# Side work between attention steps: where variances, output projections and a sort's operations stand in the queues

## The chip, the cores and the metric

The kernel runs on one core of one Trainium2 chip, in one launch. The metric is the time on the device in microseconds. The time before is the median of nine runs. One execution was also recorded by the profiler, and every duration below comes from it.

## The reference

The input has B = 2 images of C = 256 channels and 56 x 56 places, that is N = 3136 tokens of 256 numbers each, all float32. The computation, cut to what matters:

```python
x = relu(batchnorm(conv_nonlocal(x)) + x)         # layer 0: grouped non-local block
t = to_tokens(x)                                  # (2, 3136, 256)
q, k, v = split(layernorm(t) @ W_attn)            # 4 heads of 64
att = softmax(causal(q @ k.T / 8))
t = t + (att @ v) @ W_proj                        # causal attention
z = layernorm(t)
p = softmax(z @ gate_w + gate_b)                  # 8 experts
w, e = top_k(p, 2)                                # two experts for each token
t = t + sum(w[j] * (gelu(z @ W1[e[j]]) @ W2[e[j]]) for j in (0, 1))
```

## The kernel before

**Stages.** Layer 0 takes the first 100 us or so. Then comes causal attention, about 775 us, first over batch 0 and then over batch 1. The last 455 us are the experts' stage: tokens are sorted by expert, and 102 blocks of 128 rows go through their expert's two matrices, batch 0's blocks first.

**Attention.** Queries are cut into 7 blocks of W = 448 (index i). The four heads go in two pairs (hp). So each batch has 14 sections, written here (b, i, hp), and 28 in all. Within a section, `attend` walks over the key chunks j of 128 keys that the causal mask leaves. One key chunk is one step:

- `scores` (L669) makes a tile `sc` on TensorE (PE). ScalarE (ACT) takes its exponential into `st` (L677). If the chunk lies on the diagonal, VectorE (DVE) multiplies the edge by a 0/1 mask (L679). DVE adds `st` to a running sum `acc` (L687 for the first, L691 for the rest).
- `values` (L709) multiplies `st` by the values into `yp`, three steps later (`LAG = 3`).

Steps on the diagonal ("cut" in the code) have fewer columns, and each is followed by a full step as long as there are some. They stand at a section's end. `sc` has two buffers, `st` five.

When the scores of a section's last step have been issued, `visit(i, hp)` runs, then `sum_rows`, whose four matmuls `sp` (L733) sum `acc` over the partitions. The sums go out and back through DRAM on SP's queue (L741, L744), are inverted (L753, L754), broadcast (L759) and multiplied into the head's result (L765); `later` holds these tasks with the step at which they are due. At the start of the next section GpSimd (POOL) adds the two halves of `yp` (L721).

**Work at a visit.** `ahead` gives the projections for the next query block as pieces: after hp = 0 four `query_key` pieces (qk, L549) with the copies of `qT` and `kT` (L557), after hp = 1 up to four `value` pieces (v, L566, copies L575); and the transposes of normalised tokens (xp, L535, copied to `px` at L541; POOL normalises them, L520) for the block after that. After batch 0's last block these are pieces of batch 1. Each piece of PE takes a PSUM bank from `pm`, which has two, used in turn; so does `sp`. A piece therefore waits until the piece two before it has been copied out.

**Side work.** For each batch a generator `tokens` yields between pieces: `project_gate` once; `project_out`, which for two chunks of 128 tokens multiplies the attention's result by W_proj (pp, L619), adds it to the tokens on DVE (L624), stores them for batch 0 (L626) and takes mean and variance (`stats`, L177 and L178); then `dispatch`, the sort by expert: Newton steps for the reciprocal deviation (L998 to L1001), softmax, two largest, ranks and slots, some 60 small DVE operations, and at last 25 scatters: DVE makes the rows (L1303), POOL issues two indirect DMAs for each (L1311). `bg` gives these rows two buffers. After batch 0's sort the experts' first matrices are loaded (L1795). `apart` and `op` in `dispatch` only yield.

A generator yields `True` after work, `False` where it must wait for something, and `"pe"` just before work for PE. `pull(n)` advances the first generator in `queue` that can go on, until n of them have yielded `True`; one that yields `"pe"` is held back until `products()` advances it. With `every=True`, in the experts' stage, `"pe"` is passed over. The manual schedule issues instructions in just this order on each engine; each engine works through its queue in order.

Before, every second step calls `pull(2)`, and a visit is: all projections, then twice `pull()` and `products()`, then the transposes, then `sp`.

Of the kernel before, what the change touches and what calls it, by code (L numbers as in the profile page):

```python
# [28 lines left out]
def conv_attn_moe_kernel(  # L29
# [52 lines left out]
    P = 128  # L82
    B, C, N = x.shape
# [8 lines left out]
    NCH = -(-N // P)  # L92
    W = 448
# [79 lines left out]
    def stats(b, n, m, k, pool, nm):  # L173

        for a in range(m):
            st6 = pool.tile([P, 6], F32, tag="st6", name=f"st6_{nm}_{n}_{a}")
            nc.vector.bn_stats(st6[:k], ts[b][:k, n + a, :C])  # L177
            nc.vector.bn_aggr(ts[b][:k, n + a, MEAN : MEAN + 2], st6[:k])  # L178
# [9 lines left out]
    with tc.tile_pool(name="c_w", bufs=1) as cw, tc.tile_pool(name="c_s", bufs=2) as cs, tc.tile_pool(  # L188
# [170 lines left out]
        first = fold(0, gram(0, iter(())))  # L359
# [98 lines left out]
    def layer1(nm, general):  # L458

        with ExitStack() as whole:  # L460
# [4 lines left out]
            bg = pool(whole, "bg", bufs=2)  # L465
# [143 lines left out]
            def project_out(b, qT, done):  # L609

                for first, m, k in pairs():
                    while done() < (first + m - 1) * P + k:
                        yield False
                    yield "pe"
                    for n in range(first, first + m):
                        o = n * P
                        ps = bank(f"pp_{b}_{n}")
                        for c in range(NH):
                            nc.tensor.matmul(  # L619
                                ps[:k, : C + E], qT[:, c, o : o + k], wpr[:, c, :],  # L620
                                start=(c == 0), stop=(c == NH - 1),
                            )
                        t = ts[b][:k, n, : C + E]
                        nc.vector.tensor_tensor(t, t, ps[:k, : C + E], ALU.add)  # L624
                        if b == 0:
                            nc.sync.dma_start(out=rest_d[:k, n], in_=t[:, :C])  # L626
                    stats(b, first, m, k, bg, f"o{nm}{b}")

                    for _ in range(3 if b else 1):
                        yield True  # L630

            def attend(
                b, qT, kT, v, fst, fs, psc, py, visit, between, clock, later, finished
# [4 lines left out]
                steps, firsts = [], {}  # L638
                for i in range(NB):
                    nk = -(-((i + 1) * W) // P)  # L640
                    whole_js = [j for j in range(nk) if (j + 1) * P - 1 <= i * W]
                    cut = [j for j in range(nk) if j not in whole_js]
# [136 lines left out]
                for n in range(len(steps) + LAG):  # L779
                    if 0 < n <= len(steps) and steps[n - 1][4]:  # L780
                        i, hp = steps[n - 1][:2]
                        visit(i, hp)
                        sum_rows(hp, i)
                    if n < len(steps):
                        i = steps[n][0]
                        between(i, ends[i] - n)

                    late = n >= LAG and steps[n - LAG][3]
                    if n >= LAG:
                        due(clock[0])  # L790
                        clock[0] += 1
                    if n >= LAG and not late:
                        values(n - LAG)
                    if n < len(steps):
                        scores(n)
                    if late:
                        values(n - LAG)
# [154 lines left out]
            def dispatch(b):  # L952

                t = ts[b]
                tail = chunk(NCH - 1)
                ops = [0]

                def small_piece():

                    if b:  # L960
                        yield True
# [5 lines left out]

                def op():

                    ops[0] += 1  # L970
                    for _ in range(0 if b else 1 + ops[0] % 2):
                        yield True

                def small(name, last=E, dt=F32):
# [2 lines left out]
                def wide(ap):  # L977
# [8 lines left out]
                    small(k, 1).rearrange("p t o -> p (t o)") for k in ("newton_x", "newton_y", "red")  # L986
                )
                nc.vector.tensor_scalar(x, var, 1e-5, None, ALU.add)
                nc.vector.tensor_scalar(
                    y.bitcast(I32), x.bitcast(I32), 1, None, ALU.arith_shift_right  # L990
                )
                nc.vector.tensor_scalar(
                    y.bitcast(I32), y.bitcast(I32), -1.0, float(0x5F3759DF), ALU.mult, ALU.add
                )
                yield from small_piece()
                for i in range(4):
                    to = var if i == 3 else y
                    nc.vector.tensor_tensor(z, y, y, ALU.mult)  # L998
                    nc.vector.tensor_tensor(z, z, x, ALU.mult)
                    nc.vector.tensor_scalar(z, z, -0.5, 1.5, ALU.mult, ALU.add)  # L1000
                    nc.vector.tensor_tensor(to, y, z, ALU.mult)  # L1001
                    yield from op()
                    yield from small_piece()
# [28 lines left out]
                left = small("left")  # L1032
# [77 lines left out]
                first = few("first")  # L1110
# [187 lines left out]
                for n in range(NCH):  # L1298
                    kk = chunk(n)
                    xr = (scatter_rows[0] if b else bg).tile(  # L1300
                        [P, width], F32, tag="xr", name=f"xr_{nm}{b}_{n}"
                    )
                    nc.vector.tensor_scalar(  # L1303
                        xr[:kk, :C], t[:kk, n, :C],
                        t[:kk, n, MEAN : MEAN + 1], t[:kk, n, RSTD : RSTD + 1],
                        ALU.subtract, ALU.mult,
                    )
                    if b:
                        nc.vector.tensor_copy(xr[:kk, C:], t[:kk, n, C + E - 2 : SLOT + 1])  # L1309
                    for k in range(2):  # L1310
                        s = nc.gpsimd.indirect_dma_start(  # L1311
                            out=xds[b],
                            out_offset=bass.IndirectOffsetOnAxis(ap=idxs[b][:kk, k, n : n + 1], axis=0),
                            in_=xr[:kk],
                            in_offset=None,
                            bounds_check=xds[b].shape[0] - 1,
                            oob_is_err=False,
                        )
                        group = f"x_slots_{nm}{b}"
                        tc.declare_no_dep(s.ins, group=group, reason="different rows")  # L1320
                        tc.add_to_no_dep_group(group, s.ins)
                        if b or k:
                            yield True
                    if b == 0:
                        yield False
                sent[b] = True

            def experts(w1s, w2s, b2s, ex, es, ps6, between, need, written, settle, decide):
# [420 lines left out]
            def advance(g):  # L1749
                held.discard(g)  # L1750
                r = next(g, None)
                if r is None:
                    queue.remove(g)
                elif r == "pe":
                    held.add(g)
                return r

            def pull(n=1, every=False):

                while n > 0:  # L1760
                    for g in list(queue):
                        if g in held and not every:
                            continue
                        r = advance(g)
                        while r == "pe" and every:
                            r = advance(g)
                        if r is None or r is True:
                            n -= r is True
                            break
                    else:  # L1770
                        return

            def products():

                for g in list(queue):
                    if g in held:
                        advance(g)
                        return
# [88 lines left out]
            else:  # L1867
# [26 lines left out]
                for b in range(B):  # L1894
                    queue.append(tokens(b, qT, lambda b=b: min(finished[b])))

                    def visit(i, hp):

                        now, then = ahead(b, i, hp)
                        for piece in now:  # L1900
                            piece()
                        for _ in range(2):
                            pull()
                            products()
                        for piece in then:
                            piece()

                    def between(i, left):
                        if b == B - 1 and i == NB - 1:

                            now = load_w2(left < NCH - 4)
                            for _ in range(1 if left > NCH - 4 else 2):
                                next(now, None)

                        tick[0] += 1
                        if tick[0] % 2:
                            pull(2)

                    due = attend(
                        b, qT, kT, v, fst, fs, psc, py, visit, between,  # L1920
                        clock, later, finished[b],
                    )
# [250 lines left out]
```

## Time and profile before

| | |
|---|---|
| median of 9 runs | 1330.9 us (1328.14 to 1336.74) |
| profiled execution, its own time | 1331.52 us |
| its span, first to last instruction | 1329.8 us |
| mean granted TensorE clock | 0.991 |
| layer 1's attention | about 100 to 875 us |
| the experts' stage | about 875 to 1330 us |
| batch 0's scatters (L1303) | 689.7 to 776.0 us |

Times in the profile count from the first instruction. A line of a group or of the timeline names the source line, the engine, the operation, what it writes and reads, and in brackets how long the engine stood idle before it and what ended that.

### The profile page before, as it was taken

What the parts mean: (1) busy time and instruction counts of PE and PEld (TensorE: products, weight loads), DVE (VectorE), ACT (ScalarE), POOL (GpSimd) and SP (SyncE); (2) the same over time, 40 slices, a digit from 0 to 9 for tenths busy, and PEclk for the clock granted to TensorE, in tenths of its full rate; (3) what the DMA queues carried; (4) which work ended last, traced back from release to release, by engine and by line L of the source; (5) the groups of instructions that cost most, each with busy time, mean ns of one, the idle gap of its engine ahead of it and who ended that gap; (6) DMA issues with size and microseconds to landing.
All of it is one profiled execution on the core that took longest, in us unless ns stands there. A gap on an engine that the chain in (4) does not pass through costs nothing. (4 is left out here: it accounts for less than half of the span.)

```text
span 1329.8 us, 28093 instructions
## 1 busy us (share of the span) xinstructions
PE 1272.5 (96%) x10589; PEld 829.6 (62%) x10589; DVE 795.2 (60%) x1665; ACT 609.7 (46%) x1227; POOL 349.4 (26%) x317
## 2 busy tenths in 40 slices
PE   8998999999999999999999899999999899899997
PEld 7875445544444555444444344579978799798896
DVE  1582567667777745766877687764754343354564
ACT  0144555555656554555554456543422233243442
POOL 1112330000002223311126630000066212665561
PEclk9999999999999999999999999999989899899999
DMA  9994101000000001000002233321244333465554
GB/s 296 384 350 133 23 17 32 24 9 24 9 16 9 25 1 28 21 16 9 16 23 81 73 138 96 103 72 54 67 134 140 116 112 97 144 186 184 178 172 132
DMA packets 111182, 124.49 MB, mean 94 GB/s; under 512 B 19686, under 2 KB 100823, under 8 KB 111040
## 3 DMA queue, kind: packets, MB, share of 16 engines
q1 hardware_dynamic: 97216, 93.44, 22.8%
q0 software_dynamic: 9840, 25.67, 5.7%
q10 hardware_dynamic: 3984, 3.50, 0.8%
q8 instruction: 87, 1.43, 0.4%
q14 instruction: 55, 0.45, 0.1%
HBM read 62.71 MB, written 61.05 MB: 93 GB/s over the span
## 5 line engine op out<-in xcount | busy, mean ns | idle before, releaser
L677 ACT ACTIVATE st_f<-sc_f 128x896 f32<-128x896 f32 (+5 forms) x400 | 330.5, 840 | 226.0 <-PE sc_f L669 194.3
L691 DVE TENSOR_TENSOR acc_f<-acc_f,st_f 128x896 f32<-128x896 f32 (+5 forms) x372 | 379.9, 1021 | 73.4 <-ACT st_f L677 58.8
L669 PE MATMUL sc_f<-qT_f,kT_f 64*64 64x448 f32 (+6 forms) x3184 | 340.4, 500 | 10.1 <-ACT st_f L677 7.2
L709 PE MATMUL yp_f<-st_f,v_f 64*64 64x448 f32 (+6 forms) x3184 | 342.1, 501 | 4.0 <-DVE st_f L679 2.6
L1442 ACT ACTIVATE g_f<-ht_f,b1b 128x128 f32<-128x128 f32 x408 | 116.9, 371 | 255.6 <-PE ht_f L1433 123.3
L669 PEld LDWEIGHTS sc_f<-qT_f,kT_f 64*64 64x64 f32 x3184 | 121.1, 133 | 164.8 <-issue 122.9
L709 PEld LDWEIGHTS yp_f<-st_f,v_f 64*64 64x64 f32 x3184 | 120.3, 133 | 156.7 <-issue 133.7
L1433 PE MATMUL ht_f<-xT_f,w_f 128*128 128x128 f32 x1632 | 207.2, 278 | 9.9 <-issue 8.8
L1433 PEld LDWEIGHTS ht_f<-xT_f,w_f 128*128 128x128 f32 x1632 | 200.5, 194 | 18.3 <-issue 13.0
L721 POOL TENSOR_TENSOR qT_f<-both_f 128x448 f32<-128x448 f32 x28 | 37.0, 1321 | 493.0 <-ACT both_f L720 492.9
L1311 POOL DMA_INDIRECT x_slots<-xr_f,idx x100 | 111.0, 1110 | 146.2 <-DVE xr_f L1309 101.5
L1421 DVE COPY w_f<-w1s_f 128x1024 f32 x102 | 72.1, 708 | 90.2 <-PE ht_f L1433 35.3
L520 POOL TENSOR_SCALAR xn_f<-t 128x256 f32<-128x256 f32 (+1 forms) x50 | 80.3, 1612 | 171.3 <-PE xp_f L535 66.2
L1473 POOL DMA_INDIRECT y_tokens<-ys_f,to_f x57 | 58.2, 1021 | 128.9 <-DVE ys_f L1462 103.9
L1462 DVE TENSOR_TENSOR ys_f<-yp_f,kT_f 128x128 f32<-128x128 f32 x102 | 29.6, 290 | 101.8 <-PE yp_f L1452 74.9
L549 PE MATMUL qk_f<-px_f,wat 128*128 128x512 f32 (+2 forms) x224 | 88.1, 546 | 1.2 <-ACT px_f L541 1.2
L549 PEld LDWEIGHTS qk_f<-px_f,wat 128*128 128x128 f32 x224 | 40.6, 190 | 46.9 <-issue 41.6
L679 DVE TENSOR_TENSOR st_f<-st_f,keep 128x256 f32<-128x256 f32 (+1 forms) x112 | 45.6, 407 | 34.4 <-ACT st_f L677 33.2
L687 DVE COPY acc_f<-st_f 128x896 f32<-128x896 f32 x28 | 17.7, 634 | 79.4 <-ACT st_f L677 79.1
L1452 PE MATMUL yp_f<-kT_f,g_f 128*128 x204 | 62.3, 387 | 1.3 <-issue 1.3
L1452 PE MATMUL yp_f<-px_f,g_f 128*128 x204 | 62.4, 388 | 0.9 <-issue 0.7
L1452 PE MATMUL yp_f<-v_f,g_f 128*128 x204 | 61.5, 383 | 0.9 <-issue 0.9
(273 smaller groups left out, 1270.3 us busy)
## 6 DMA issues: line engine op xcount, KB each, us to landing
x_slots<-fill SPq DMA_DIRECT2D x1, 8190.0 KB
xb_f<-x_slots SPq DMA_DIRECT2D x60, 130.0 KB
x_slots<-fill SPq DMA_DIRECT2D x1, 7296.0 KB
y_slots<-ys_f SPq DMA_DIRECT2D x57, 128.0 KB
kept<-t SPq DMA_DIRECT2D x2, 3200.0 KB
x<-in_x_dram SPq DMA_DIRECT2D x14, 448.0 KB
rb_f<-inverses SPq DMA_DIRECT2D x56, 112.0 KB
xr<-in_x_rows_dram SPq DMA_DIRECT2D x12, 512.0 KB
```

What stands on the lines that cost most here:

```text
L520: nc.gpsimd.tensor_scalar(xn[:k, a], ts[b][:k, n + a, :C], ts[b][:k, n + a, MEAN : MEAN + 1], ts[b][:k, n + a, RSTD : RSTD + 1], ALU.subtr ...
L549: nc.tensor.matmul(ps[:, :w], wat[:, c, d0 : d0 + P], px[:, s % 2, c, :w], start=(c == 0), stop=(c == NH - 1),)
L669: nc.tensor.matmul(ps[h : h + HS, a, c0:W], kT[hp][rows, j * P + h : j * P + h + HS], qT[rows, hp, q0 + c0 : q0 + W], start=True, stop=True,)
L677: nc.scalar.activation(st[:k, :, c0:], ps[:k, :, c0:W], AF.Exp, scale=SCALE)
L691: nc.vector.tensor_tensor(acc[:k, :, c0:], acc[:k, :, c0:], st[:k, :, c0:], ALU.add)
L709: nc.tensor.matmul(yp[a * HS : (a + 1) * HS, h // HS, c0:W], v[hp][h : h + HS, j, a, :HS], st[h : h + HS, a, c0:], start=first, stop=bool( ...
L1311: s = nc.gpsimd.indirect_dma_start(out=xds[b], out_offset=bass.IndirectOffsetOnAxis(ap=idxs[b][:kk, k, n : n + 1], axis=0), in_=xr[:kk], i ...
L1421: nc.vector.tensor_copy(w, w1s[:, :, bass.ds(e, 1), :].rearrange("p c e h -> p c (e h)"))
L1433: nc.tensor.matmul(ht[:, k, :], w[:, c, k * P : (k + 1) * P], xT[:, c, :], start=(c == 0), stop=(c == NH - 1),)
L1442: nc.scalar.activation(g[:, k, :], ht[:, k, :], AF.Gelu, bias=b1bs[b][:, k, i : i + 1])
L1452: nc.tensor.matmul(yp[:, :C], g[:, k, :], w2s[k][:, bass.ds(e, 1), :].rearrange("p e d -> p (e d)"), start=(k == 0), stop=(k == KH - 1),)
L1473: s = nc.gpsimd.indirect_dma_start(out=y_tokens, out_offset=bass.IndirectOffsetOnAxis(ap=to[:, n % GB : n % GB + 1], axis=0), in_=ys, in_o ...
```

## The change

The order of issue changes, and nothing else: both programs hold the same instructions.

- The variances leave `project_out`. A new generator `closer` for each pair of chunks is put at the head of the queue; each pull takes one chunk's mean and variance. `project_out` ends when all are taken, and no longer yields `True` after each pair, so a second `products()` can follow at once with the next pair.
- A visit issues all but the last two projections, then `products()` once or twice, then the last but one projection, the transposes, and the last projection. It no longer pulls. Without projections (last block) `products()` stands before and after the transposes.
- `between` pulls one piece at every step, except in block i = 0, whose steps all lie on the diagonal; before, two at every second step.
- `op` in `dispatch` yields once for batch 0, where it yielded once and twice in turn; and it stands after each of Newton's operations, which went four at a time.
- After each scatter of batch 0, `dispatch` yields `True` where it yielded `False`: a scatter takes two pulls, and the next generator in the queue is not reached.
- In the experts' stage a pull passes over one `"pe"` and counts a second.

In the new order a visit reads, with a batch's two output projections as an example: qk qk pp pp pp pp qk xp qk sp, where it was qk qk qk qk pp pp pp pp xp sp.

```diff
-                    stats(b, first, m, k, bg, f"o{nm}{b}")
-
-                    for _ in range(3 if b else 1):
-                        yield True
+                    queue.appendleft(closer(b, first, m, k))
+                while unclosed[b]:
+                    yield False
+
+            unclosed = [NCH] * B
+
+            def closer(b, first, m, k):
+
+                for n in range(first, first + m):
+                    stats(b, n, 1, k, bg, f"o{nm}{b}")
+                    unclosed[b] -= 1
+                    yield True
...
-                        between(i, ends[i] - n)
+                        between(i, ends[i] - n, (steps[n][2] + 1) * P > i * W + 1)
...
                 def op():
 
-                    ops[0] += 1
-                    for _ in range(0 if b else 1 + ops[0] % 2):
+                    if b == 0:
                         yield True
...
                     nc.vector.tensor_tensor(z, y, y, ALU.mult)
+                    yield from op()
                     nc.vector.tensor_tensor(z, z, x, ALU.mult)
+                    yield from op()
                     nc.vector.tensor_scalar(z, z, -0.5, 1.5, ALU.mult, ALU.add)
+                    yield from op()
                     nc.vector.tensor_tensor(to, y, z, ALU.mult)
                     yield from op()
...
                     if b == 0:
-                        yield False
+                        yield True
...
                         r = advance(g)
-                        while r == "pe" and every:
+                        if r == "pe" and every:
                             r = advance(g)
+                            r = True if r == "pe" else r
...
                         now, then = ahead(b, i, hp)
-                        for piece in now:
+                        for piece in now[:-2]:
                             piece()
-                        for _ in range(2):
-                            pull()
+                        products()
+                        if now:
                             products()
-                        for piece in then:
+                        for piece in now[-2:-1] + then + now[-1:]:
                             piece()
-
-                    def between(i, left):
+                        if not now:
+                            products()
+
+                    def between(i, left, cut):
...
                         tick[0] += 1
-                        if tick[0] % 2:
-                            pull(2)
+                        if not cut or i:
+                            pull()
```

More of the change, by code (lines that the diff above doesn't have):

```diff
@@ L955, in dispatch @@
                 tail = chunk(NCH - 1)
-                ops = [0]
                 def small_piece():
@@ L998, in dispatch @@
                     nc.vector.tensor_tensor(z, y, y, ALU.mult)
+                    yield from op()
                     nc.vector.tensor_tensor(z, z, x, ALU.mult)
+                    yield from op()
                     nc.vector.tensor_scalar(z, z, -0.5, 1.5, ALU.mult, ALU.add)
+                    yield from op()
                     nc.vector.tensor_tensor(to, y, z, ALU.mult)
```

## The prediction

> **What bounds the kernel now.** I read busy time and the chain of waits first, then the clock by windows, then what PE waits for. The chain ends at an ACT copy with 0% shares, so it tells nothing. Busy time does:
>
> ```profile
> PE 1272.5 (96%) x10589; PEld 829.6 (62%) x10589; DVE 795.2 (60%) x1665; ACT 609.7 (46%) x1227; POOL 349.4 (26%) x317
> ```
>
> PE bounds the kernel, and the change neither adds nor removes an instruction on any engine: in the order of the two programs each line occurs equally often, on equal shapes. Only PE's idle time can move. Windows by stage (PE, PEld, DVE, ACT, POOL busy, clock, DMA):
>
> ```profile
> 100.00:500.00 400.00, 392.40 (x3740) 191.55 (x3739) 251.85 (x373) 222.65 (x343) 65.08 (x43) 1.00 0.09 27
> 500.00:690.00 190.00, 183.48 (x1736) 87.50 (x1738) 131.03 (x249) 103.10 (x168) 36.10 (x22) 1.00 0.07 16
> 690.00:800.00 110.00, 101.14 (x1014) 44.25 (x1006) 79.64 (x125) 55.31 (x79) 62.06 (x52) 1.00 0.28 95
> 800.00:875.00 75.00, 73.85 (x800) 35.52 (x792) 57.67 (x73) 43.08 (x52) 2.49 (x2) 1.00 0.30 88
> 875.00:1330.00 455.00, 428.97 (x2847) 391.69 (x2843) 225.30 (x682) 161.97 (x540) 168.94 (x161) 0.97 0.42 131
> ```
>
> The first four are attention: 775 us with 24.1 us idle at full clock. The last is the experts' stage, 26 us idle, with three stretches of 6.8 us at clock 0.50 (989.1:995.9 and two more); of the change only the second batch's projections and sort reach it, one block of tokens sooner or later. Attention's waits:
>
> ```profile
> PE sc_f L669 <- ACT st_f L677: 7.2, 8, 1.5
> PE yp_f L709 <- DVE st_f L679: 2.6, 5, 1.0
> PE sp_f L733 <- DVE t L624: 2.3, 3, 1.2
> PE xp_f L535 <- DVE t L624: 2.2, 6, 1.2
> PE sc_f L669 <- issue: 1.7, 3, 0.9
> PE sp_f L733 <- ACT kT_f L557: 1.5, 6, 0.3
> PE sp_f L733 <- ACT v_f L575: 0.9, 3, 0.3
> ```
>
> A wait costs more than it prints. Score matmuls print 0.98 us but the next values start 0.75 us later (453.33 to 454.08), so 0.16 to 0.23 us of modelled tail hides part of each; I add 0.16.
>
> Write (b,i,hp) for a section: batch, query block, head pair; its visit follows it.
>
> **Bunched sort and variances, gain 0.9.** At visit (1,1,1) DVE receives 22 side operations in a row:
>
> ```profile
> 548.13 0.42 DVE L177 BATCH_NORM_STATS2 st_of<-t 64x6 f32<-64x256 f32 x1
> ...
> 549.45 0.19 DVE L998 TENSOR_TENSOR red_f<-newton_y_f 128x25 f32<-128x25 f32 x1
> ...
> 550.21 0.76 DVE L624 TENSOR_TENSOR t<-t,pp_f 128x264 f32<-128x264 f32 x2
> 550.77 0.63 PE L535 MATMUL xp_f<-ident,xn_f 128*128 128x128 f32 x4 [1.16 <-DVE t L624]
> ```
>
> L624 empties the PSUM bank that the transposes need. Variances and Newton steps stand ahead of it, seven of Newton's at 0.19 alone. After, the three L624 come first and variances follow one chunk a step: 1.16 + 0.16 = 1.3 goes. Next late is the last value product (below), 0.4 (0.3 + 0.16, less what overlaps). Gain 0.9. What hides the moved variances is DVE's slack in full steps: 1.50 us of PE against 1.09 of L691, 0.41 for 0.56 (starts 548.13 to 548.59, and the aggregate); the 0.15 short per step falls into the lag of three steps between scores and values. Without it: 0.15 a step, up to 4 steps in eight visits, 5.
>
> **Projections amid the others, 0.2.** Five other visits put transposes behind L624: (2.2 - 1.2) / 5 = 0.2, with tail 0.36 each. Four of these go, since no variance stands between the L624s any more; (0,6,0) has no input projection and keeps its own. But bank order decides what comes: two banks alternate, and with one transpose pair (about 0.5 us) between the last two projections, the last waits for the copy of the one before it: kT 0.25 (1.5 / 6) + 0.16 = 0.4, v 0.3. Three visits exchange 0.36 for 0.4, one for 0.3, and (1,4,1) its sum's wait for px, 0.4 + 0.16, for 0.3: 0.2. Behind the new wait stand, on PE, the sum and the next section's values and scores, and for those ACT waits; so it costs in full. The other two of sp's waits on L624 (2.3 - 1.2 = 1.1, at (1,6,0) and (1,6,1)) become those of a third projection, two pairs standing there now: 0.
>
> **Transposes before the last projection, none, then -0.7.** Where no output projection stands, the sum (sp) waits 0.4 or 0.3 today because transposes are shorter than the copy; after, the last projection waits the same for the same reason. At (0,6,1) two transpose pairs come before the last value: two waits, 0.3 more each way, I take -0.4. Visit (1,5,1) loses its projections, and its sum then follows a value product, as at (0,5,1): -0.3. Moving the gate's transposes and product to two visits removes wg's 0.7 + 0.16 and adds two copies' waits of 0.4: 0.
>
> **Sorting on diagonal steps, gain 2.3.** In sections (1,2,0) to (1,4,1) values wait for the masked tile:
>
> ```profile
> 642.96 0.62 DVE L765 TENSOR_TENSOR qT_f<-qT_f,rb_f 128x448 f32<-128x448 f32 x1
> 643.49 0.42 DVE L679 TENSOR_TENSOR st_f<-st_f,keep 128x256 f32<-128x256 f32 x1
> 643.97 0.66 PE L709 MATMUL yp_f<-st_f,v_f 64*64 64x256 f32 x8 [0.66 <-DVE st_f L679]
> ```
>
> Sum 2.6 + 5 x 0.16 = 3.4. The order shows in (1,2,0) four Newton operations ahead of one mask become one; in (1,3,0) three wide ones (L1042, L1045, L1047: 0.36, 0.36, 0.8) leave the diagonal and L1021 (0.35) comes; in (1,3,1) 0.36 + 0.59 leave and 0.36 + 0.36 + 0.8 come earlier, so its wait stays; (1,4,0) gains some. I leave 1.1: gain 2.3, from -1 to 3.4.
>
> **Scatter, gain 2.9.** 25 pieces (L1303 on DVE, two L1311 on POOL at 0.97 + 0.30) went one per two steps plus up to two a visit; now one per two steps only, 25 in 48 steps. At 690-800 scores wait 5.1 us for ACT in six places; one cause is in the DVE queue:
>
> ```profile
> 757.06 0.41 DVE L1303 TENSOR_SCALAR xr_f<-t 128x256 f32<-128x256 f32 x1 [2.38 <-DMA x_slots<-xr_f,idx]
> 757.87 0.59 PE L733 MATMUL sp_f<-acc_f,ones 128*32 128x224 f32 x8 [1.19 <-DVE t L624]
> ```
>
> L1303 waits for its buffer, and the projections, then the sum, wait behind it. Visit (1,5,0) has no projection now, nor extra pieces: 1.19 + 0.16 = 1.35 goes. Of the six waits (6.1 with tails) I let 1.5 go, from -3.5 (a diagonal more inside the scatter) to 4 (POOL drained during each visit). Instruction waits ("issue") stay.
>
> **SP, -0.4.** w1's eight loads of 512 KB move from (1,5,1) into (1,6,0), spread by two steps. Behind two of them and five of w2 queue the broadcasts that L765 needs; that wait was 1.6 us and cost PE nothing. Bounds 0 and -2. The last is issued at step 17 of (1,6,0), about 50 us before the experts begin at 875. SP's other issues keep their order but for one pair of stores of rest, one section later. Projections moved into the experts' stage cost PE the same there, on other banks' slack: 0.
>
> **Sum.** 0.9 + 0.2 - 0.7 + 2.3 + 2.9 - 0.4 = 5.2. The profiled execution took 1331.5 us (span 1329.8), 0.6 above the median of 1330.9: 1331.5 - 5.2 = 1326.3, and, set against the median, a little under it. I say 1326.
>
> [...] An operation of 25 elements took 1.13 us, six times its usual, beside POOL's addition:
>
> ```profile
> 556.68 1.25 POOL L721 TENSOR_TENSOR qT_f<-both_f 128x448 f32<-128x448 f32 x1 [12.82 <-ACT both_f L720]
> 556.84 1.13 DVE L998 TENSOR_TENSOR red_f<-newton_y_f 128x25 f32<-128x25 f32 x1
> ```
>
> [...] By the rows L721 comes in full steps, where DVE has 0.41 us to spare and three steps of lag, and already catches L691 there (1.4 us in most sections) without a wait of PE; I charge nothing.
>
> **Rivals.** *Waits change places only* (0.30): the bank waits are an exchange, and the diagonals keep theirs because L765 and the mask meet as before. Left is 1.35 + 0.9 - 0.7 = 1.55: 1330. For it: (1,3,1). Against it: the 22 operations are gone from a visit. *Scatter unloads* (0.15): no visit pieces, L1303 never waits for its buffer, all of the 6.1 but 0.5 goes instead of 1.5: 1326.3 - 4.1 = 1322. *Slower: POOL falls behind on diagonals* (0.17). Place: (1,5,0), and (1,5,1), whose diagonal had no scatter. A piece takes POOL 2.5 us, 3.8 where L1311 prints 1.6; a diagonal pair gives 1.72 to 2.6 us of PE. Four pairs short by 1 to 2 us, in two or three diagonals, put L1303's wait ahead of the mask in DVE's queue: 8 to 10 us on top of 1326.3: 1335.5. It decides once L1303 waits over 9 us in all (now 4.0). That the change does not do what it says is ruled out by the order.
>
> **Chances.** About 0.3% (4.0 us) is what a measurement can tell from no change. Forecast 0.38, for itself 1323 to 1327; with the unloaded scatter 0.53 faster; 0.30 within; 0.17 slower. The range runs from the scatter's upper bound with the mask waits all gone (1331.5 - 5.2 - 2.5 - 1.1 - 2 of bank waits = 1320.7, and 1 for its other ends) to the slower rival.
>
> **What would show it.** Right: no xp wait over 0.5 us on L624; yp on L679 near 1 us; qk and v waits on ACT copies in place of sp's; DVE's idle time on x_slots under 4 us. Wrong: L1303 waits growing in (1,5,1), L765 over 3 us late near 815, or a fourth half-clock stretch among the experts (each costs 3.4 us, half of 6.8).

## The result, and the profile after

The changed kernel took 1338.2 us (median of 16 runs) against 1329.9 for the kernel before (53 runs): ratio 1.0057, 95% interval 1.004 to 1.0073. One of the 16 runs took 7328 us and is left out of the ratio. The changed kernel is slower by 7.6 us by the ratio and by 8.3 by the medians, where about 5 less were forecast. The profiled execution took 1335.8 us, span 1334.1, clock 0.989; it is 4.3 above the one of before, and 2.4 below its own median.

Busy time on the page of the changed kernel, first: PE is busy 4.8 us longer with the same instructions, and its idle time (span less busy time) is 56.8 us against 57.3. So a list of waits cannot show the whole loss. A part stands in work that took longer, as at half the clock (ahead of PE's last instruction 23.9 us at clock 0.50 against 20.5), or as at the breaks that e1_tail and e2_visit_only measure (0.2 us a visit).

```profile
PE 1277.3 (96%) x10589; PEld 834.3 (63%) x10589; DVE 788.8 (59%) x1665; ACT 608.2 (46%) x1227; POOL 350.2 (26%) x317
```

The same windows as in the prediction (PE, PEld, DVE, ACT, POOL busy, clock, DMA):

```profile
100.00:500.00 400.00, 392.31 (x3735) 189.97 (x3734) 250.59 (x373) 221.71 (x341) 63.47 (x43) 1.00 0.09 26
500.00:690.00 190.00, 186.34 (x1738) 87.67 (x1740) 123.82 (x237) 104.24 (x170) 39.02 (x22) 1.00 0.06 16
690.00:800.00 110.00, 102.38 (x1058) 46.63 (x1054) 81.63 (x123) 58.74 (x83) 61.30 (x53) 1.00 0.25 82
800.00:875.00 75.00, 73.07 (x761) 36.88 (x751) 55.48 (x74) 40.70 (x51) 2.29 (x2) 1.00 0.35 110
875.00:1330.00 455.00, 430.31 (x2844) 393.43 (x2842) 227.61 (x694) 159.39 (x537) 169.38 (x161) 0.97 0.41 130
```

Attention's idle time fell from 24.1 to 20.9 us, 2.9 of it in 500:690, where the diagonals with the sort are. Its waits answer to the prediction's marks:

```profile
PE sc_f L677 <- ACT st_f L685: 5.8, 7, 1.8
PE qk_f L549 <- ACT kT_f L557: 2.6, 10, 0.3
PE v_f L566 <- ACT v_f L575: 1.2, 4, 0.3
...
PE xp_f L535 <- DVE t L624: 0.7, 1, 0.7
PE yp_f L717 <- DVE st_f L687: 0.6, 2, 0.4
```

The mask waits (yp) went from 2.6 to 0.6 us, those of xp on L624 from 2.2 to 0.7, and waits of the projections qk and v stand in place of the sum's. All this was forecast, but for the one xp wait that is left, 0.7, which is above the mark of 0.5. Yet attention ends (last sum's matmul) at 870.9 us instead of 873.0, and 1.8 of these 2.1 us are one pair of output projections less in it (8 matmuls, one started every 0.22 us). So attention as such gained 0.3. The loss lies after it.

It shows at block 41 of the experts (counted from 0). Ahead of this block's matmuls PE has the transposes of block 42, the first whose rows come from both batches; here and below, block 41 "starts" with them. They need the second batch's sort and its 50 scatters on POOL. The timeline of the changed kernel there:

```profile
1051.32 0.91 POOL L1323 DMA_INDIRECT x_slots<-xr_f,idx  x1 [0.31 <-issue]
...
1053.93 1.44 SPq L1363 DMA_DIRECT2D xb_f<-x_slots  x3
...
1055.34 1.95 PE L1445 MATMUL ht_f<-xT_f,w_f 128*128 128x128 f32 x16
...
1059.54 0.96 DVE L1399 TENSOR_TENSOR xb_f<-xb_f,xo_f 128x768 f32<-128x768 f32 x1 [1.87 <-DMA y_slots<-ys_f]
...
1060.60 0.66 PE L1422 MATMUL tp_f<-ident,xb_f 128*128 128x128 f32 x2 [3.31 <-issue]
```

After the last scatter (1051.32 + 0.91) come the load of the rows, DVE's addition (ends 1060.50), and 0.1 us later PE's transposes, which had waited 3.31. The label "issue" hides that: the addition is what the transposes read. In the kernel before PE did not wait there:

```profile
1043.52 0.91 POOL L1311 DMA_INDIRECT x_slots<-xr_f,idx  x1 [0.30 <-issue]
...
1052.95 0.96 DVE L1387 TENSOR_TENSOR xb_f<-xb_f,xo_f 128x768 f32<-128x768 f32 x1
...
1057.39 0.38 PE L1410 MATMUL tp_f<-ident,xb_f 128*128 128x128 f32 x2
```

There the addition ended 3.5 us before PE came. The chain is 6.6 us later in the changed kernel (1060.5 against 1053.9): 3.5 of room are used up and 3.2 become a later block (1060.6 against 1057.4). From there to the end the two profiles differ by 1.1 us, and 3.2 + 1.1 = 4.3.

Yet the change did not put the sort later among PE's work. The sort's first product on PE, `rank`, stands ahead of block 18 in both programs, with the same work left behind it. First the kernel before, then the changed one:

```profile
951.14 0.61 PE L1070 MATMUL rank_f<-both_f,keep 128*128 128x200 f32 x2 [0.52 <-DVE both_f L1059]
```

```profile
956.53 0.60 PE L1082 MATMUL rank_f<-both_f,keep 128*128 128x200 f32 x2 [1.59 <-DVE both_f L1071]
```

From attention's end that is 78.2 and 85.7 us. From `rank` to block 41 PE took 106.3 us before and 104.1 after, the wait of 3.31 included, and from `rank` to the end 378.7 and 377.5. So the wait at block 41 stands where PE lost as much in other ways before, and the loss is complete at `rank`: -2.1 in attention, 7.5 from there to `rank`, -1.1 behind it, 4.3 in all.

Of the 7.5 us I find 7.3: the moved pair 1.8; a wait of 2.0 at the experts' start; a half-speed stretch of 3.41 us that follows it, 1.7 (half of it); a bank wait between two pairs in a row, 0.74; and 1.06 more of waiting for the rank's operand (PE's loss there, from start to start, went from 0.69 to 1.75). The first wait, the stretch (a line of windows as above) and the bank wait:

```profile
879.56 0.20 DVE L761 RECIPROCAL back_f<-sums 128x7 f32<-128x7 f32 x1 [5.20 <-DMA sums<-sums]
879.75 0.69 DVE L1433 COPY w_f<-w1s_f 128x1024 f32 x1
...
880.59 2.51 PE L1445 MATMUL ht_f<-xT_f,w_f 128*128 128x128 f32 x16 [1.96 <-DVE w_f L1433]
...
881.96:885.37 3.41, 3.41 (x18) 3.41 (x18) 0.65 (x2) 1.40 (x5) 0.00 (x0) 0.50 0.53 179
...
890.53 2.05 PE L619 MATMUL pp_f<-wpr,qT_f 128*128 128x264 f32 x8 [0.55 <-DVE t L624]
```

The weight copy stands in DVE's queue behind a reciprocal that waits for attention's last sums. Before, a pair of output projections kept PE busy just then (880.56 to 882.5).

### The profile page after: what moved, and what is told of

The parts are those of the page before. It is cut to its first block, busy times and chain, and to the rows that moved or that the text cites. A ratio compares the mean times of both kernels' runs of the same rounds, so it can differ in the third digit from the quotient of the medians.

```text
span 1334.1 us, 28054 instructions
## 1 busy us (share of the span) xinstructions
PE 1277.3 (96%) x10589; PEld 834.3 (63%) x10589; DVE 788.8 (59%) x1665; ACT 608.2 (46%) x1227; POOL 350.2 (26%) x317
## 4 chain that ended last, share of the span: by engine, by line
PE 88%; DVE 3%; ACT 3%; issue 2%; DMA 2%; another core or an unknown queue 1%; SPq 0%; DVEq 0%; ACTq 0%
PE yp_f L717 19%; PE sc_f L677 19%; PE ht_f L1445 13%; PE yp_f L1464 13%; PE qk_f L549 6%; PE v_f L566 3%; PE cp L339 3%; PE pp_f L619 3%; PE gram L270 3%; PE tp_f L1422 2%; ACT st_f L685 1%; PE sp_f L741 1%; DMA y_tokens<-fill 1%; DVE acc_f L699 1%
## 5 line engine op out<-in xcount | busy, mean ns | idle before, releaser
L699 DVE TENSOR_TENSOR acc_f<-acc_f,st_f 128x896 f32<-128x896 f32 (+5 forms) x372 | 378.7, 1018 | 60.5 <-ACT st_f L685 48.8
L549 PE MATMUL qk_f<-px_f,wat 128*128 128x512 f32 (+2 forms) x224 | 92.1, 552 | 4.2 <-ACT kT_f L557 2.6
L1464 PE MATMUL yp_f<-w2s_f,g_f 128*128 x204 | 62.6, 389 | 1.0 <-issue 1.0
```

What stands on the lines that cost most here:

```text
L549: nc.tensor.matmul(ps[:, :w], wat[:, c, d0 : d0 + P], px[:, s % 2, c, :w], start=(c == 0), stop=(c == NH - 1),)
L699: nc.vector.tensor_tensor(acc[:k, :, c0:], acc[:k, :, c0:], st[:k, :, c0:], ALU.add)
L1464: nc.tensor.matmul(yp[:, :C], g[:, k, :], w2s[k][:, bass.ds(e, 1), :].rearrange("p e d -> p (e d)"), start=(k == 0), stop=(k == KH - 1),)
```

## Experiments

Theories. **A**: transposes between two projections cost PE time at every visit. **B**: the wait at the experts' start and what follows it. **C** (rival): half-speed stretches and instruction waits among the experts, shuffled by any new order. **D**: the change's effect on the steps is a real gain. **E**, formed only after the first eight runs, when e5 and e9 had gone against B: the second batch's sort sets the time of block 41, so that a gain ahead of it does not count unless the sort starts sooner. The runs came in three groups (e1 to e5, e6 to e9, e10 to e13), each on one chip, next to the kernel before. The chips were of two kinds: in the first and third group the kernel before took 1332.3 and 1331.2 us, in the second 1292.3; so ratios are compared, and traces on one kind of chip.

**e1_tail.** In the changed kernel:

```diff
-                        for piece in now[-2:-1] + then + now[-1:]:
+                        for piece in now[-2:] + then:
```

> The changed kernel, but with its transposes after the last projection again (projections, output projections amid them, transposes, sum); all else as changed. Theory A (each pair of transposes between two projections breaks PE's stream twice, about 0.1 us a break, 0.2 in some 22 visits): attention ends about 4 us earlier than in the changed kernel (last sum's matmul at 866.5 instead of 870.6), the total about 1334. Theory B (the loss sits at the experts' start, where a copy of weights waits behind the last sums' reciprocal and no output projection covers it): attention may move, but the 2.0 us wait of the expert matmul on the weight copy stays; total near 1338 less what A gives. Rival C (the cause is the clock's half-speed stretches and instruction waits among the experts, which any new order shuffles): total unchanged at 1338 within 2.

Measured: 1334.1 us, ratio 1.0006 (0.9989 to 1.0023), that is 4 under the changed kernel; attention's end 867.6. Section by section, up to (1,4,0), 0.2 us comes back in each of 19 visits, 3.7 in all. Theory A holds. But block 41 starts at 1060.6 in this profile too, with a gap of 3.65 us ahead of it: the 3.3 gained in attention were not seen there. This one profile (1337.1 us, 3.0 above the median of its kernel) does not show where the median's 4 us came about.

**e2_visit_only.** In the kernel before:

```diff
-                        for piece in now:
+                        for piece in now[:-1]:
...
-                        for piece in then:
+                        for piece in then + now[-1:]:
```

> The kernel before with one edit: at each visit the last projection is issued after the transposes. Theory A: 0.2 us more in each visit that has both, so attention ends 4 us later (last sum's matmul at 876.7 instead of 872.7), total 1330 + 4 = 1334. Where an output projection stood before the transposes, the wait for its bank may shrink a little: then 3 instead of 4. Theories B and C: no change, 1330, since neither the experts' start nor the sort moves.

Measured: 1334.7, ratio 1.003 (1.0014 to 1.0046); attention's end 877.5, later by 4.5. Up to (1,4,0), four of the visits with an output projection ahead of the transposes lost nothing, and 15 others 0.2 each. The PE timeline of visit (1,2,0), first of the kernel before, then of the changed one:

```profile
575.11 0.60 PE L535 MATMUL xp_f<-ident,xn_f 128*128 128x128 f32 x4
575.95 0.59 PE L733 MATMUL sp_f<-acc_f,ones 128*32 128x224 f32 x8 [0.24 <-ACT kT_f L557]
576.46 0.98 PE L709 MATMUL yp_f<-st_f,v_f 64*64 64x448 f32 x8
```

```profile
574.91 0.60 PE L535 MATMUL xp_f<-ident,xn_f 128*128 128x128 f32 x4
575.75 1.99 PE L549 MATMUL qk_f<-px_f,wat 128*128 128x512 f32 x4 [0.24 <-ACT kT_f L557]
577.66 0.59 PE L741 MATMUL sp_f<-acc_f,ones 128*32 128x224 f32 x8
```

The printed wait, 0.24, is the same. But four projection matmuls follow each other at 0.43 us (4 x 0.43 = 1.72) and here the sum starts 1.91 after the first: the first projection after the wait takes 0.53 to the next one, and the last 0.52 to the sum. Both are 0.1 more. In the kernel before the sum stood right behind the wait and paid neither. In e2's profile PE also waits 2.3 us ahead of block 41, with the experts' stage of the kernel before.

**e4_scatter_false.** In the changed kernel, after each scatter of the first batch:

```diff
-                        yield True
+                        yield False
```

> The changed kernel, but a scatter of the first batch again yields False, as before: a scatter takes one pull, the next generator is reached, and output projections of the second batch come in attention from (1,4,1) on, two pairs a visit, so that 10 instead of 30 of their product groups are left to the experts' stage and its sort starts 3.5 blocks sooner. My prediction's step (scatter gains 2.9 by its thinner spread): the sections (1,4,1) to (1,6,0) get slower by about 3 beside the moved projections. Theory B: two waits at the experts' start (2.0 on the weight copy, 1.7 on the rank) change, the first stays because no projection stands between the second and the third expert matmul group; total by -1 to -3 against 1338. Rival C: 1338 within 2.

Measured: 1336.2, ratio 1.0035 (1.001 to 1.006). Sections (1,4,1) to (1,6,1) took 7.0 us more than in the kernel before, with four pairs (7.1) more in them; the changed kernel 2.9 less with one pair (1.8) less. Net that is 0.2 and 1.1 under the kernel before: of my 2.9 the thinner spread shows at most 0.9. Block 41 waits no longer (the addition ends 3.5 us ahead), but it starts no sooner: a projection waits 2.4 for the last head's scaling (L773), and PE's path comes to 1061.6. The sort started seven blocks sooner (`rank` ahead of block 11), where 3.5 were expected.

**e5_recip_later.** In the changed kernel, the closing tasks of attention:

```diff
-                        for _ in range(2 * 2 if wait > 4 else 0):
+                        for _ in range(2 * 2 if wait > 4 else 2):
```

> The changed kernel, but the reciprocal of attention's last sums is issued two pulls later among the experts, behind the third copy of weights instead of ahead of it. Theory B: the expert matmul's wait of 2.0 us at 880.6 goes, and with it the half-speed stretch of 3.41 us that follows at 882 (1.7 us): total 1338 - 3.7 = 1334.5, attention's end unchanged at 870.6. Theory A and rival C: no more than the 2.0 of the wait itself, 1336 to 1338.

Measured: 1338.1, ratio 1.0054 (1.0033 to 1.0074). The wait at 880.6 and its stretch are gone, and the time is unchanged: theory B missed the total. But the edit did not leave the rest alone. It also put the second sort two blocks back (`rank` ahead of block 20), the addition for block 41 ends at 1062.9, later than in the changed kernel, and the block starts 0.1 us behind it. And the granted clock was lower: 0.986 in this profile against 0.989 in the changed kernel's. By an estimate from span and clock, some 19 us went to a clock below 1 here and some 14 there, and 17.0 against 14.5 as means of the runs. What took the gain, the later sort or the clock, is not shown.

**e6_steps_only** and **e7_rate_only**, both from the kernel before; e6 has both edits, e7 the first alone:

```diff
-                        if tick[0] % 2:
-                            pull(2)
+                        if not cut or i:
+                            pull()
...
-                    ops[0] += 1
-                    for _ in range(0 if b else 1 + ops[0] % 2):
+                    if b == 0:
                         yield True
...
+                    yield from op()        # after each of Newton's operations
```

> The kernel before with only the parts of the change that act on the steps: Newton's operations one to a pull, op once instead of once and twice in turn, and one pull at each step instead of two at every second (none in block 0). Visits, variances, scatter's yield and the experts' pull stay as before. Theory D (the diagonals' waits for the mask come from side operations bunched by pairs; my prediction's 2.3): sections (1,2,0) to (1,4,1) shorter by 2.3 to 3, attention's last sum at about 869.7 against 872.7, the experts' stage as before: total 3 us below the kernel before. Rival (the diagonals' gain needs the variances out of the visits, or the thinner scatter): less than 1 us in those sections, total unchanged.

> The kernel before with only one pull at each step instead of two at every second (none in block 0); Newton's operations stay in fours. It parts theory D in two: if the pairs of pulls are the cause, it gains nearly all of what both together gain (2.3 to 3); if Newton's fours and the doubled op are, the masks in (1,2,0) still wait (1.8 us there) and only (1,3,0) and (1,3,1) gain, 1.5. Total 1.5 to 3 below the kernel before; the experts' stage as before.

Measured on the faster kind of chip: both 1290.2 against 1292.3, ratios 0.9986 (0.9977 to 0.9995) and 0.9983 (0.9974 to 0.9992). D holds in the sum, and one pull a step makes nearly all of it: up to (1,4,0) the two are 2.1 and 1.7 us ahead of the kernel before (whose sections up to there took the same in e9, on the same chip as e6 and e7). Of e6's 2.1, though, 1.2 came in (1,1,1), ahead of the sections that D named. A gap of 2.7 us in e6 and of 2.1 in e7 stands ahead of block 41.

**e9_cover_moved.** In the kernel before, after the visit's two pulls:

```diff
+                        if b and not now and hp:
+                            pull(3)
+                            products()
```

> The kernel before with one edit: one pair of output projections moves from the experts' start (between the second and the third group of expert matmuls) into the last visit. No work is added. Theory B: the third group then waits 2.0 us for its weight copy, which stands on VectorE behind the reciprocal that awaits the last sums' way through memory; and the last visit's second pair waits 0.7 for its bank: total 2 to 3 above the kernel before, more if a half-speed stretch follows the idle time. Rival C (only clock and instruction waits differ): unchanged within 1.

Measured: 1288.9, ratio 0.9976 (0.9966 to 0.9986), faster. Theory B said slower: on this chip the weight copy made PE wait 0.4, not 2.0. E, formed after it, fits the gain: the sort starts a block sooner than in e6 and e7, the addition ends 1.2 us before PE reaches block 41, and the 2 us gap of its two neighbours is absent.

**e8_tail_single.** The changed kernel as in e1_tail, and in `pull`:

```diff
                         if r == "pe" and every:
-                            r = advance(g)
-                            r = True if r == "pe" else r
+                            r = True
```

> The changed kernel with transposes after the last projection again, and in the experts' stage a pull that meets the marker ahead of an output projection counts at once, so that pairs come singly and not two in a row. Theory A: attention's end as with the transposes alone put back (867.6). Theory B': two pairs in a row wait for each other's bank (2.7 us once where only the transposes were put back, 0.6 in the changed kernel); singly, that wait goes, but the wait of 2 us on the weight copy stays, and the second sort comes one block later: total 1 to 2 under the 1334 of the transposes alone put back. Rival C: 1334.

Measured: 1302.1, ratio 1.0075 (1.0061 to 1.0088), the slowest of all, where a gain on e1_tail was expected. The pairs come singly, and the sort two blocks later (`rank` ahead of block 20). Its timeline, POOL, DVE, PE:

```profile
1029.62 0.91 POOL L1323 DMA_INDIRECT x_slots<-xr_f,idx  x1 [0.30 <-issue]
...
1035.56 0.16 DVE L1388 TENSOR_TENSOR eq_f<-xb_f,sid 128x3 f32<-128x3 f32 x1 [13.53 <-DMA xb_f<-x_slots]
...
1038.10 0.96 DVE L1399 TENSOR_TENSOR xb_f<-xb_f,xo_f 128x768 f32<-128x768 f32 x1 [1.97 <-DMA xo_f<-x_slots]
...
1039.16 0.66 PE L1422 MATMUL tp_f<-ident,xb_f 128*128 128x128 f32 x2 [12.13 <-DVE xb_f L1399]
```

Here the label names the chain openly, and its price is 12.13 us.

**e13_after_again, e11_after_early, e12_tail_early, e10_steps_early.** e13 is the changed kernel without an edit. e11 adds two pairs in each of the last two visits, e12 also the edit of e1_tail; e10 is e6 with one more pair in each of these visits:

```diff
# e11 and e12, at the end of visit
+                        for _ in range(2 if b and not now else 0):
+                            products()
# e10, after the visit's two pulls
+                        if b and not now:
+                            for _ in range(1):
+                                pull(3)
+                                products()
```

> The changed kernel once more, beside the three other runs of this call on the same chip, since runs of the kernel before differ by 40 us from chip to chip (1332 and 1292). Theory E (the second batch's sort sets the time: its output projections, ranks and 50 scatters on GpSimd must be done before the first block that holds rows of both batches, block 41; in the changed kernel this chain ends 6.6 us later than before and TensorE waits 3.3 us there): 7 to 8 us above the kernel before, and a wait ahead of block 41 of 3 us on the slow kind of chip, 6 to 9 on the fast kind. Theory A alone (transposes between projections): 4.4 less 3 for the steps, so 1 to 2 above the kernel before.

> The changed kernel with two more pairs of output projections in each of the last two visits: 14 instead of 30 product groups are left to the experts' stage and the second sort starts three blocks sooner; no work is added, and each further pair waits 0.7 us for its bank. Theory E: the wait ahead of block 41 goes; on the slow kind of chip 1 to 3 us below the changed kernel, on the fast kind 4 to 8 below. Theory A alone: as the changed kernel or 2 to 3 slower (four bank waits).

> The same with the transposes after the last projection again (both repairs of the changed kernel at once). Theories A and E together: 3.4 below the run with the earlier projections alone, because attention's gain is no longer taken back at block 41: between the kernel before and 2 us above it on the slow kind of chip, 1 to 3 below it on the fast kind. Theory A without E: 3.4 below the changed kernel and no more.

> The kernel before with the parts of the change that act on the steps (as in the run with the steps only) and one more pair of output projections in each of the last two visits, so that the second sort starts three blocks sooner. Theory E: the steps' 3 us, of which TensorE gave 2.7 back ahead of block 41, now reach the end, and so does what the kernel before itself waits there: 3 below the kernel before on the slow kind of chip, 5 to 6 on the fast kind. Without E: 2 below on either.

| kernel | us | ratio to before (interval) | attention's end | `rank` ahead of block | addition ends | block 41 starts |
|---|---|---|---|---|---|---|
| before (its own profile) | 1331.2 | 1 | 873.0 | 18 | 1053.9 | 1057.4 |
| e13 | 1337.5 | 1.005 (1.0028 to 1.0071) | 873.5 | 18 | 1062.4 | 1064.5 |
| e11 | 1330.9 | 0.9999 (0.9979 to 1.002) | 877.6 | 15 | 1053.6 | 1057.1 |
| e12 | 1326.6 | 0.9974 (0.9956 to 0.9993) | 874.8 | 15 | 1050.7 | 1054.1 |
| e10 | 1325.1 | 0.9958 (0.994 to 0.9975) | 874.3 | 15 | 1051.4 | 1054.9 |

Four pairs moved by a few tens of us, with no work added or removed, take 6.6 us off the changed kernel (1337.5 to 1330.9); its attention ends 4 us later than in e13 with these pairs in it, and all the same block 41 starts 7 sooner. With the transposes last another 4.3 us go. e10 beats both kernels, by 0.4% and 0.9%. In its trace, as in e11's,

```profile
1052.69 0.96 DVE L1399 TENSOR_TENSOR xb_f<-xb_f,xo_f 128x768 f32<-128x768 f32 x1
...
1057.13 0.38 PE L1422 MATMUL tp_f<-ident,xb_f 128*128 128x128 f32 x2
```

the addition is done 3.5 us before the transposes (lines of e11).

E had the signs right and the sizes wrong: it said 1 to 3 us below the changed kernel for e11 (measured 6.6), 0 to 2 above the kernel before for e12 (4.6 below), 3 below it for e10 (6.1). And the wait of 3 us that it expected ahead of block 41 in e13 is absent: there the addition ends 2.1 us before the transposes start. Between the profiles of e13 and e11, 7.7 us apart, 2.9 stand in attention, 4.1 between its end and `rank`, and 0.7 behind `rank` (an estimate, with the moved work taken out at 0.22 us a matmul and 3.73 a block). So e11's gain need not come through the sort: fewer projections left among the first blocks also meet fewer waits there. In e13 a bank wait of 2.1 and a weight copy of 1.7 stand in that stretch, in e11 weight copies alone, 1.3 and less.

**Where the loss stands.** The five profiles on the slower kind of chip with `rank` ahead of block 18:

| profile | order among the experts | attention's end to `rank` | PE's wait ahead of block 41 | `rank` to the end |
|---|---|---|---|---|
| before | before | 78.2 | 0 | 378.7 |
| e2 | before | 78.6 | 2.3 | 374.1 |
| changed | changed | 85.7 | 3.3 | 377.5 |
| e13 | changed | 87.0 | 0 | 376.2 |
| e1 | changed | 87.6 | 3.7 | 380.2 |

The stretch to `rank` goes with the order of issue: 7.5 to 9.4 us more, of which the moved pair's work is 1.8 (e6 and e7, with the order of before, have 78.2 too). The wait ahead of block 41 does not, and neither does the time behind `rank`. That the sort can hold PE up is shown all the same: in seven of the fourteen profiles (these three with a wait, and e5 to e8) PE's transposes start 0.10 us after the addition, and with `rank` ahead of block 17 or sooner (e4, e9 to e12) they never wait. That it makes the difference between the two kernels is not shown.

Rival C: by an estimate from spans and mean clocks of all runs, the time lost to a clock below 1 is 14.0 us in e13 and 14.1 in the kernel before next to it, so the clock makes no part that shows of the difference between these two. It is 11.4 in e11, so that of its 6.3 us of mean gain over e13 some 2.6 came through the clock and 3.7 at full speed; each of these has a standard error of about 1.

## Why the prediction was wrong

- **Bunched sort and variances, sorting on diagonals: right.** 0.9 + 2.3 = 3.2 was forecast. In e1_tail, where the transposes' price is taken out, sections (1,1,1) to (1,4,0) are shorter than in the kernel before by 3.5 us.
- **The 1.13 us beside POOL's addition: charged nothing, rightly.** An operation of 25 elements beside POOL's addition took 1.13 us in the changed kernel again (L1013 at 582.9), and no wait of PE follows it.
- **Gate, and the exchange of bank waits: right in kind.** Ten qk waits and four of v carry what the sum's waits carried.
- **Transposes before the last projection: mis-sized.** I took none, then -0.7, since "the last projection waits the same for the same reason". The wait is the same, but the wait now falls on a projection, and a sum follows a projection: 0.2 in each visit with both, 3.7 up to (1,4,0). e1_tail and e2_visit_only show it from both sides. This is about as much as bunching and diagonals gained.
- **Scatter, 2.9: wrong.** e4_scatter_false puts the old yield back and loses 0.9 at most. Most of what I read as the scatter's price is not the order's at all: in e9_cover_moved, which issues the same instructions in (1,5,0) and (1,5,1) as the kernel before, these sections are shorter by 7.8 and 3.4 us on the other kind of chip.
- **The step that failed most**: "Projections moved into the experts' stage cost PE the same there, on other banks' slack: 0." From attention's end to `rank` the changed kernel took 7.5 us more, and the moved pair's own work is 1.8 of them. The other 5.7 I put at nothing: 2.0 of waiting for a weight copy, where the pair that stood there before had kept PE busy, and 1.7 for the half-speed stretch that follows; 0.74 for the bank between two pairs in a row; 1.06 ahead of `rank`; 0.2 not found. I had read PE's busy time as the only bound and did not ask what a pair covers where it stands. e13 and e1 repeat the longer stretch. e11, with four pairs taken out of that stage, gives 6.6 us back, some 2.6 of it through the clock.
- **The sort that comes "one block of tokens sooner or later"** got no price either. It has one, since block 41 needs the last of 50 scatters, which take POOL 79 us from the first to the last (972.8 to 1052.2, of which it waits 13 for rows from DVE): two blocks later, in e8_tail_single, PE waited 12.1 us, against 2.1 and 2.7 in e7 and e6 on the same chip. But between the kernel before and the changed one the sort did not move among the blocks, and the profiles do not show that it made a difference there.
- **The rivals.** None had this mechanism. The marks of my slower case, POOL behind on diagonals, did not appear: L1303 (now L1315) waited 3.0 us in all, and L765 (now L773) not at all up to 830 us, where I charged 0.4. One mark of being wrong did: five half-speed stretches ahead of PE's last instruction instead of three, 23.9 us in all instead of 20.5.
- **The sum.** By the two profiles attention gained 0.3 (the moved pair's work taken out) instead of 5.2, the experts' start lost 5.7 instead of 0, and 1.1 came back behind `rank`: 4.3 slower. The medians say 8.3, and 6.3 in e13: the profiled run of before lies 1.6 above its median, that of the changed kernel 2.4 below, and what makes up these 4.0 is open. With both repairs, the transposes last and four pairs sooner (e12), the change is by the medians 4.6 us faster than the kernel before.

## What to carry to other kernels

A stage in which one engine is 95% busy (here PE, 430 of 455 us among the experts) can still have other chains with a few us of room (3.5 ahead of block 41 in the kernel before). Before giving a moved operation the price of nothing, ask what it covered where it stood; then follow what it produces to the first instruction of the busy engine that reads it, and compare the two times there. A wait late in a trace need not be the loss: find an instruction behind which both programs have the same work left, and see whether they are apart there already. A wait that only changes its place is not free either: what stands right behind it, and what follows that, may run slower than what stood there before (0.1 us each at visit (1,2,0)). And small gains may add up: e6 (0.14%) and e9 (0.24%) on the faster kind of chip, 0.42% for both sorts of edit together in e10 on the slower. Whether one makes the other worth more is not shown.

## What the runs showed of the hardware

- Two kinds of chips: the same kernel took 1331 to 1332 us in two groups of runs and 1292 in another. In the profile of before, PE waits 13.7 us among the experts for "issue" (8.8 + 2.9 + 1.6 + 0.4); in e9's, from the faster kind of chip, PE's waits there name no "issue" at all, and the granted clock is 1.00 in every window up to 1130 us (0.97 from 875 to 1130 in the profile of before) and 0.99 behind it. What makes the chips differ is not shown. The changed kernel itself ran on the slower kind alone.
- In the profiles of before and after, the granted clock was 0.50 in eight stretches ahead of PE's last instruction, 6.83 us each in the three of before, 3.41, 6.83, 3.41, 6.83 and 3.41 in the five of after, and 1.00 between them. PE was idle for 1.4 to 2.9 us of the 5 us ahead of each; but 2.0 us of it in 5 also passed without one (1006.6 to 1011.6 in the kernel before). So an exposed wait can cost more than it lasts. Behind the wait of 1.96 at the start of the changed kernel's experts a pair of transposes took 0.64 us instead of 0.38; behind one of 1.73 at the same place in e1_tail such a pair took 0.38. In e8_tail_single the pair right behind the wait of 12.1 took 0.66, pairs ahead of it 0.38, and the granted clock over 1000:1130 was 0.95, where e6 and e9 have 1.00.
